# Half-row matmul pieces, a split cell and a new written order in a row-LSTM kernel

## The chip, the cores and the metric

The kernel runs on one core of one Trainium2 chip. The metric is the device time of one execution in microseconds (us), as the median of several executions. The engines are called as the profile calls them: PE (TensorE matmul) with PEld (its weight loads), DVE (VectorE), ACT (ScalarE), POOL (GpSimd) and SP (SyncE, which issues the DMAs).

## The reference

The input x has 8 images of 96 channels, 128 rows and 128 columns, in fp32. It is group-normalised (32 groups), a masked 1x3 convolution turns each row into 4x96 gate inputs, and an LSTM runs down the 128 rows. Its state h is convolved along the row with a full 3-tap kernel. The output is x plus h.

```
its = conv(gn(x), W_is * mask) + b_is            # 1x3, causal mask
def step((h, c), row):
    gates = conv1d(h, W_ss) + b_ss + row         # 3 taps, 96 -> 384
    f, i, o = sigmoid(three of the four parts);  g = tanh(the fourth)
    c = f * c + i * g
    h = o * tanh(c)
out = x + h of all rows
```

Row r cannot begin its convolution of h before row r-1 has ended its output product.

## The kernel before

**Half steps.** The 8 images are two halves of 4 (s = 0 and 1). One row of one half is a half step, numbered n = 2*row + s, so there are 256. Half step n needs h of half step n-2. The two halves alternate, so that the pointwise work of half step n-1 can lie beside the matmuls of half step n.

**Products.** A half step has three PSUM banks, A, B and C (128 output channels each, 512 fp32 columns: even columns in the lower 256, odd ones in the upper 256). The 3-tap convolution is written as four products per bank on sums and differences of neighbouring columns: "1" takes `vs` (even plus odd), "2" takes `vf` (odd minus even), "0" and "3" take `vd` (two shifted differences). They contract over all 128 rows (96 channels of h and 32 of x). The remaining 64 channels of x come in as three "own" products per bank, P, Q and E, which contract over 64 rows: their operand `xs` and weights lie twice in SBUF, in rows 0-63 and in rows 64-127, and `own` picks one of the two copies by bank and half. All are made by `mm` (line 393), 256 columns each; each product is recorded as two weight loads and two matmuls[...].

**Pointwise work.** `copy` (cp) takes product 1 out with the bias; `even` (lo) and `odd` (hi) combine it with product 2 within the bank, on DVE; products 0, E and 3 are added to that by PE. Then `tanh` (ta) and `sigmoid` (si) run on ACT for each bank; `forget` (fg, f*c), `gated` (gt, i*g), `cell` (ce, the sum) on DVE, `cell_tanh` (th) on ACT, `output` (ou, o*th into `hx`) on DVE. From `hx`, `difference` (F, line 503) and `total` (S, line 499) on DVE and `shifted` (D, line 507) on POOL make the operands `vf`, `vs` and `vd` of half step n+2. `residual` (re) on POOL adds h to x. POOL also normalises the next block's rows (`work`, called from `finish`), and `finish` issues the stores and loads of a block of four rows on SP's queue.

**What sets the order.** PE, ACT, DVE and POOL are under a manual schedule: each engine runs its instructions in the order in which the text `PERIOD` (line 586) names them, with `PRODUCTS` (line 590) in place of X for the own products. `do` (line 607) reads the text. A mark ' means half step n-1, + means n+1, * means n+2. So in one period the products of half step n are on PE while the cell of n-1 is on ACT and DVE, and ou', F', S' and D' come while PE does the own products. Semaphore waits between the engines are put in by the framework.[...]

**The tail.** The last half step (lines 837 to 847) already does `cell`, `cell_tanh` and `output` in two parts of two images each.

Of the kernel before, what the change touches and what calls it, by code (L numbers as in the profile page):

```python
# [8 lines left out]
AF = mybir.ActivationFunctionType  # L9
# [12 lines left out]
def kernel(  # L22
# [32 lines left out]
    nc = tc.nc  # L55
    B, C, H, W = x.shape
    P = 128
    NH = 2
    BH = B // NH
# [4 lines left out]
    C2 = 64  # L64
# [21 lines left out]
    wt = [tap[1], wm[:, 0, :], wm[:, 1, :], tap[2]]  # L86
    wo = [wx[:, 0, :], wx[:, 1, :], tap[3]]
# [73 lines left out]
    E = mybir.EngineType  # L161
# [5 lines left out]
    def bank(name):  # L167
        return ps_pool.tile([P, 512], F32, tag="ps", name=name)
# [57 lines left out]
    class Scale:  # L226


        def __init__(self, s, lo, hi, banks=None):
            n, self.name = hi - lo, f"{s}_{lo}"  # L230
            self.st, self.rstd, self.nmr = (
                st[s][:, lo:hi], rstd[s][:, :, lo:hi], nmr[s][:, :, lo:hi]
            )


            self.first, at = banks is None, 0 if banks is None else 3 * BH
            self.banks = banks or [bank(f"{name}{self.name}") for name in ("dm", "pv")]
            self.dm, self.pv = (
                own[:, at : at + i * n].rearrange("p (i b) -> p i b", i=i)
                for own, i in zip(self.banks, (3, 2))  # L240
            )
            self.pm = self.dm[:, 1:3, :]
            self.q, self.t, self.minus = (
                const.tile([P, *shape], F32, name=f"{name}{self.name}")
                for name, shape in (("q", [n]), ("t", [2, n]), ("minus", [2, n]))
            )
            for i in range(2):
                self.mm(self.pv[:, i, :], i, eps[:, 0:n], start=self.first and i == 0)

        def mm(self, o, i, rhs, start=False, stop=False):  # L250
            nc.tensor.matmul(o, gm[:, i, :], rhs, start=start, stop=stop, skip_group_check=True)
# [104 lines left out]
    last = NT * NH - 1  # L356
    order = {"A": 0, "B": 1, "C": 2}

    def gt(n, s, row, shape=(C, 2 * HB)):
        return g_pool.tile(list(shape), F32, tag=n, name=f"{n}_{s}_{row}")  # L360

    class HalfStep:


        def __init__(self, n):
            self.n, (self.row, self.s) = n, divmod(n, NH)
            self.ps, self.m1, self.moving, self.done, self.gates = {}, {}, {}, set(), None
            self.started, self.images = set(), {}
            self.hx = hx[self.s][self.row // R % 2][:, self.row % R]
            self.xs = xs[self.s][self.row // R % 2][:, self.row % R]  # L370
            self.c = cs[self.s].rearrange("p t b j -> p (t b j)")
# [14 lines left out]
        def mm(self, a, half, weights, rhs, rows=slice(0, P)):  # L386
            self.take_bank(a)
            new = a not in self.started
            self.started.add(a)

            lo, hi = self.images.get(a, (0, BH))
            cols = slice(lo * J, hi * J)
            nc.tensor.matmul(  # L393
                self.ps[a][:, bass.ts(half, HB)][:, cols],
                weights[rows, bass.ts(a, P)],
                rhs[rows, cols],
                start=new,
                stop=False,
                skip_group_check=True,
            )  # L400

        def own(self, a, i):

            low = a == order["A"] or (a == order["C"] and (self.s == 0 or (self.n, i) == (1, 2)))
            rhs = self.xs[:, i].rearrange("p b j -> p (b j)")
            self.mm(a, i % 2, wo[i], rhs, slice(0, C2) if low else slice(C2, P))

        def p_(self, a):
            self.own(a, 0)
# [5 lines left out]
        def t_(self, a):  # L415
            if 2 * self.row + self.s == last:
                self.mm(a, 0, wh, self.xs[:, 2].rearrange("p b j -> p (b j)"))
            else:
                self.own(a, 2)

        def m1_(self, a):
            self.mm(a, 0, wt[1], self.moving["vs"][:, 0])

        def m2_(self, a):
            self.mm(a, 1, wt[2], self.moving["vf"][:, 0])

        def m0_(self, a):
            self.mm(a, 0, wt[0], self.moving["vd"][:, 1])

        def m3_(self, a):  # L430
            self.mm(a, 1, wt[3], self.moving["vd"][:, 0])

        def copy(self, a):
            self.m1[a] = self.tile(f"m{a}", (P, HB))
            m1, column = self.ps[a][:, 0:HB], bias[:, a : a + 1]
            if a == order["A"] and self.n not in (0, 2):
                nc.vector.tensor_scalar(self.m1[a], m1, column, None, ALU.add)
            else:
                nc.scalar.activation(self.m1[a], m1, AF.Identity, bias=column)  # L439

        def even(self, a):
            nc.vector.tensor_add(self.ps[a][:, 0:HB], self.m1[a], self.ps[a][:, HB:])  # L442

        def odd(self, a):
            hi = self.ps[a][:, HB:]
            nc.vector.tensor_sub(hi, self.m1[a], hi)  # L446

        def tanh(self, a):
            nc.scalar.activation(self.g[a * 32 : (a + 1) * 32], self.ps[a][C:P], AF.Tanh)  # L449


        def sigmoid(self, a):
# [7 lines left out]
            if self.row > 0:  # L460
                nc.vector.tensor_mul(f, f, self.c)  # L461

        def gated(self):
            to = self.g if self.row > 0 else self.c
            nc.vector.tensor_mul(to, self.ps[1][0:C], self.g)


        def part(self, ap, lo, hi):
            return ap.rearrange("p (t b j) -> p t b j", t=2, b=BH)[:, :, lo:hi]
# [4 lines left out]
                nc.vector.tensor_add(c, f, g)  # L474

        def cell_tanh(self, lo=0, hi=BH):
            if lo == 0:
                self.th = self.tile("th")
            nc.scalar.activation(self.part(self.th, lo, hi), self.part(self.c, lo, hi), AF.Tanh)  # L479

# [60 lines left out]
    def shared(s, k, *images):  # L541
        return [(normalise_shared, nc.gpsimd, s, k, j, 0, R) for j in images]
# [12 lines left out]
    def work(n):  # L555
        if n < len(FIRST):
            return FIRST[n]
        row, s = divmod(n, NH)
        k, r = divmod(row, R)
        parts = []  # L560
        if r == R - 1 and k + 2 < NB:
            parts.append((own_image, s, k + 2, 0))
        elif r < R - 1 and k + 1 < NB:
            parts.append((own_image, s, k + 1, r + 1))
        if k + 1 < NB:
            parts += shared(s, k + 1, *SHARED[r])
        if r == R - 2 and k + 2 < NB:
            parts.append((load_rows, s, k + 2))
        return parts

    def finish(n):
        for part, *args in work(n):
            part(*args)
        row, s = divmod(n, NH)
        k, r = divmod(row, R)
        if r == R - 1:
            store(s, k, R - 1 if k + 1 == NB else 0, R)
            if k + 2 < NB:
                load(s, k + 2)
        elif r == R - 2 and k + 1 == NB:  # L580
            store(s, k, 0, R - 1)
# [2 lines left out]


    PERIOD = (
        "2A 1A siB' fg' 2B taB' cpA 1B loA 3C' cpB hiA 0C' loB 1C taC' hiB 2C siC' 0A gt'",
        "3A cpC ce' 0B loC th' hiC", "X", "ou' F' S' D' re'", "3B taA siA",
    )
    PRODUCTS = (  # L590
        "P+A P+B Q+A Q+B P+C P*A Q+C EA EB EC",
        "Q+A P+B P+C Q+B Q+C EB EA EC",
    )
    PARTS = {
        "P": "p_", "Q": "q_", "E": "t_", "1": "m1_", "2": "m2_", "0": "m0_", "3": "m3_",
        "cp": "copy", "lo": "even", "hi": "odd", "ta": "tanh", "si": "sigmoid",
# [7 lines left out]
            steps[n] = HalfStep(n)  # L604
        return steps[n]

    def do(n, names):

        for name in names.split():
            at = n  # L610
            for mark, offset in (("'", -1), ("+", 1), ("*", 2)):
                if mark in name:
                    at, name = n + offset, name.replace(mark, "")
            tile_ = name[-1] if name[-1] in order else ""
            part = name[: len(name) - len(tile_)]

            if part in ("S", "F", "D"):
                at += NH
            if not 0 <= at <= last:
                continue  # L620
            step = half_step(at)
            if name not in step.done:
                step.done.add(name)
                getattr(step, PARTS[part])(*([order[tile_]] if tile_ else []))

# [117 lines left out]
    n = m = 0  # L745
    for b in range(B):
# [7 lines left out]
        for k in range(QW // CH):  # L754
# [11 lines left out]
            if alone:  # L766
                i = list(shares).index(k)
# [12 lines left out]
    rows = ring[2][:, 0 : (R - 1) * BH * (W + 1)].rearrange("p (r q) -> p r q", q=W + 1)  # L780
# [12 lines left out]
    j = BH - 1  # L793
# [8 lines left out]
    step = half_step(1)  # L802
# [25 lines left out]
    finish(0)  # L828
    do(1, "gt th 0+A 3+A 0+B 3+B 0+C 3+C ou F S D re")
    finish(1)  # L830
    do(2, "taA siA P+C P*A Q+C")
    for n in range(3, last + 1):
        for names in PERIOD if n < last else PERIOD[:1]:
            do(n, PRODUCTS[n % 2] if names == "X" else names)
            if "re'" in names.split():
                finish(n - 1)
    do(last, "3A EA cpC ce' taA siA 0B 3B EB loC hiC th' siB taB fg ou' re'")
    finish(last - 1)
    do(last, "0C 3C EC taC siC gt")
    step, halves = half_step(last), [(0, BH // 2), (BH // 2, BH)]  # L840
    for at in halves:
        step.cell(*at)
# [60 lines left out]
```

## Time and profile before

| | before |
|---|---|
| median of 3 runs | 2062.54 us (2061.33 to 2066.29) |
| span of the profiled execution | 2059.9 us; its device time beside the span is not given, the runs lie 1.4 to 6.4 us above it |
| PE busy | 1961.9 us (95%), 10888 matmuls |
| DVE busy | 1675.9 us (81%) |
| ACT busy | 1363.7 us (66%) |
| POOL busy | 1449.6 us (70%) |
| granted TensorE clock | 0.997 |

Busy time is the time in which an engine had at least one instruction running. A timeline row gives the start, the time from the start of the first to the end of the last of the merged instructions, the engine, the line, what is written and read with its shape, and the number of instructions; in brackets stands how long the engine was idle before it and what ended that. For PE's matmuls the end is modelled, and successive matmuls overlap: what counts is the distance between their starts.

### The profile page before, as it was taken

The page shows a single profiled execution, that of the slowest core. Times are in us where ns is not written, and L with a number is a line of the kernel's source. Part 1 is how long each engine was busy: PE and PEld are TensorE (multiplying, and loading weights), DVE is VectorE, ACT ScalarE, POOL GpSimd, SP SyncE. Part 2 cuts the span into 40 slices and gives each one's busy share as a digit, 9 for nine tenths or more (in the row PEclk, how much of TensorE's full clock was granted, in tenths as well). Part 3 has the DMA queues.
Part 4 walks back from the last instruction along what each step waited for, and adds up shares of the span by engine and source line. Part 5 has one row for each costly group of instructions (what it writes and reads, how often), then busy time and mean ns, then how long its engine had stood idle before and what let it go on. Part 6 is the DMA issues. An engine that isn't in the chain of part 4 may idle for free.

```text
span 2059.9 us, 31445 instructions
## 1 busy us (share of the span) xinstructions
PE 1961.9 (95%) x10888; PEld 1597.5 (78%) x10888; DVE 1675.9 (81%) x3489; ACT 1363.7 (66%) x2403; POOL 1449.6 (70%) x1652
## 2 busy tenths in 40 slices
PE   0399999999999999999999999999999999999998
PEld 0278888888888888888888888888888888888886
DVE  5778888888888888888888888888888888888887
ACT  4776666666666666666666666666666666666666
POOL 3358777777777777777777777777777777777762
PEclk9999999999999999999999999999999999999999
DMA  9994333344433334443333443333444333344411
GB/s 381 424 309 109 91 84 89 97 113 113 107 74 85 88 99 113 113 103 75 86 88 101 113 113 100 73 90 87 104 113 113 99 74 87 88 106 113 113 31 32
DMA packets 103326, 236.26 MB, mean 115 GB/s; under 512 B 5953, under 2 KB 8897, under 8 KB 97281
## 3 DMA queue, kind: packets, MB, share of 16 engines
q1 hardware_dynamic: 103168, 234.25, 41.8%
q8 instruction: 88, 1.44, 0.3%
q14 instruction: 70, 0.57, 0.1%
HBM read 183.90 MB, written 50.33 MB: 114 GB/s over the span
## 4 chain that ended last, share of the span: by engine, by line
PE 93%; DMA 3%; DVE 2%; ACT 1%; POOL 0%; issue 0%; SPq 0%; DVEq 0%; POOLq 0%
PE ps L393 93%; DMA xs<-in_x_dram 3%; DVE bst L771 1%; POOL xw L297 0%; POOL xs L315 0%; POOL xs L316 0%; ACT piece L295 0%; SPq L759 0%; ACT piece L216 0%; ACT xs L216 0%; ACT xs L217 0%; ACT piece L217 0%; ACT g L449 0%; DVE st L677 0%; ACT th L479 0%
## 5 line engine op out<-in xcount | busy, mean ns | idle before, releaser
L393 PE MATMUL ps<-vd,wl 128*128 128x256 f32 x3072 | 814.3, 388 | 0.1
L449 ACT ACTIVATE g<-ps 32x512 f32<-32x512 f32 x768 | 454.3, 592 | 450.5 <-PE ps L393 442.4
L393 PEld LDWEIGHTS ps<-vd,wl 128*128 128x128 f32 x3072 | 562.4, 190 | 151.3 <-issue 84.7
L507 POOL TENSOR_TENSOR vd<-hx 128x512 f32<-128x512 f32 x257 | 266.5, 1037 | 459.0 <-DVE vs L499 457.8
L393 PE MATMUL ps<-xs,wx 64*128 64x256 f32 x3080 | 459.9, 394 | 11.0 <-POOL xs L315 11.0
L393 PE MATMUL ps<-vs,wm 128*128 128x256 f32 x1540 | 460.6, 381 | 4.0 <-POOL vs L499 4.0
L393 PE MATMUL ps<-vf,wm 128*128 128x256 f32 x1540 | 460.4, 381 | 0.0
L456 ACT ACTIVATE ps<-ps 96x512 f32<-96x512 f32 x766 | 417.7, 572 | 16.1
L393 PEld LDWEIGHTS ps<-xs,wx 64*128 64x128 f32 x3080 | 323.9, 187 | 119.7 <-issue 83.9
L461 DVE TENSOR_TENSOR ps<-ps,c 96x512 f32<-96x512 f32 x254 | 176.6, 695 | 259.4 <-ACT ps L456 259.4
L446 DVE TENSOR_TENSOR ps<-m,ps 128x256 f32<-128x256 f32 x768 | 329.1, 429 | 27.3 <-PE ps L393 1.2
L525 POOL TENSOR_TENSOR x<-x,hx 96x512 f32<-96x512 f32 x255 | 330.5, 1296 | 5.7 <-DVE hx L486 5.7
L442 DVE TENSOR_TENSOR ps<-m,ps 128x256 f32<-128x256 f32 x768 | 324.8, 423 | 9.7 <-ACT m L439 0.9
L393 PEld LDWEIGHTS ps<-vs,wm 128*128 128x128 f32 x1540 | 293.6, 191 | 45.9 <-POOL vs L499 5.0
L393 PEld LDWEIGHTS ps<-vf,wm 128*128 128x128 f32 x1540 | 293.9, 191 | 41.1 <-POOL vf L503 0.5
L439 ACT ACTIVATE m<-ps,wl 128x256 f32<-128x256 f32 x514 | 243.9, 475 | 74.8 <-PE ps L393 61.5
L316 POOL TENSOR_TENSOR xs<-xw 128x512 f32<-128x512 f32 (+1 forms) x254 | 270.4, 1064 | 0.0
L393 PE MATMUL ps<-xs,wt 64*128 64x256 f32 x1530 | 264.6, 377 | 0.0
L479 ACT ACTIVATE th<-c 96x512 f32<-96x512 f32 (+1 forms) x257 | 161.4, 628 | 104.8 <-DVE c L474 103.8
L297 POOL TENSOR_SCALAR hx<-x,rstd,nmr 32x512 f32<-32x512 f32 (+1 forms) x252 | 204.7, 812 | 25.9
L297 POOL TENSOR_SCALAR xw<-xr,rstd,nmr 128x512 f32<-128x512 f32 x252 | 204.8, 813 | 8.1 <-DVE nmr L289 6.5
L393 PEld LDWEIGHTS ps<-xs,wt 64*128 64x128 f32 x1530 | 195.0, 187 | 18.1 <-issue 0.7
(91 smaller groups left out, 1295.2 us busy)
## 6 DMA issues: line engine op xcount, KB each, us to landing
xr<-in_x_dram SPq DMA_DIRECT2D x124, 512.0 KB, 6.7
x<-in_x_dram SPq DMA_DIRECT2D x63, 768.0 KB, 5.9
out_dram<-x SPq DMA_DIRECT2D x62, 768.0 KB, 4.9
xs<-in_x_dram SPq DMA_DIRECT2D x30, 1024.0 KB, 12.3
piece<-in_x_dram SPq DMA_DIRECT2D x16, 1024.0 KB, 12.3
x<-in_x_dram SPq DMA_DIRECT2D x62, 256.0 KB, 3.2
xs<-in_x_dram SPq DMA_DIRECT2D x4, 512.0 KB, 8.3
out_dram<-x SPq DMA_DIRECT2D x2, 576.0 KB, 3.8
```

The lines of the kernel that those rows point to most:

```text
L297: engine.tensor_scalar(dst, src, scale, shift, ALU.mult, ALU.add)
L316: nc.gpsimd.tensor_sub(differences, strided(xw[:, 0, :], 0, [(W + 1, n), (J, 2), (1, J)]), strided(xw[:, 0, :], J + 1, [(W + 1, n), (0, 2) ...
L393: nc.tensor.matmul(self.ps[a][:, bass.ts(half, HB)][:, cols], weights[rows, bass.ts(a, P)], rhs[rows, cols], start=new, stop=False, skip_g ...
L439: nc.scalar.activation(self.m1[a], m1, AF.Identity, bias=column)
L442: nc.vector.tensor_add(self.ps[a][:, 0:HB], self.m1[a], self.ps[a][:, HB:])
L446: nc.vector.tensor_sub(hi, self.m1[a], hi)
L449: nc.scalar.activation(self.g[a * 32 : (a + 1) * 32], self.ps[a][C:P], AF.Tanh)
L456: nc.scalar.activation(gate, gate, AF.Sigmoid)
L461: nc.vector.tensor_mul(f, f, self.c)
L479: nc.scalar.activation(self.part(self.th, lo, hi), self.part(self.c, lo, hi), AF.Tanh)
L507: diff = nc.gpsimd.tensor_sub(self.operand("vd", 2)[:, :, lo:hi], strided(h, 1, [(BH * JP - 1, 2), (JP, hi - lo), (1, J)]), strided(h, 0, ...
L525: (nc.gpsimd if 2 * row + s < last else nc.vector).tensor_add(xo, xo, self.h)
```

## The change

All products of h become two pieces of 64 rows each, one in rows 0-63 and one in rows 64-127, so that one half step has 24 such pieces and 9 own products, 33 in all. A small class `Lanes` gives each piece a row half in turn: an own product takes whichever half has had fewer, the second piece of a product takes the other half than the first. Before a piece that goes into a bank whose last piece was on the other row half, `lanes.wait` puts a no-operation on PE that waits for that last piece's end, unless a later piece has been waited for already.

The gate product, the cell, its tanh, the output and the tanh of bank C are made in two parts of two images ("b" is images 2 and 3, "a" is 0 and 1). The copy of bank A moves from DVE to ACT. `re` is named one period later (re''), and `work` of half step n-1 (W) no longer comes after the residual but by itself. D is named at the start of the next period (D''), S and F at the end of the period, after the output. `PRODUCTS` is gone; there is one text for all periods. The last half step's E remains a full 128-row product, as do its products 0 and 3 where neither piece has been made.

```diff
+    class Lanes:
+        ROWS = (slice(0, C2), slice(C2, P))
...
+        def take(self, first=None):
+            if first is not None:
+                self.last = 1 - self.ROWS.index(first)
+            elif self.taken[0] != self.taken[1]:
+                self.last = int(self.taken[1] < self.taken[0])
+            else:
+                self.last = 1 - self.last
+            self.taken[self.last] += 1
+            return self.ROWS[self.last]
...
+        def wait(self, number):
+
+            if number > self.waited:
+                tc.add_manual_dep(
+                    nc.tensor.nop().ins,
+                    self.made[number].ins.name,
...
+                self.waited = number
...
             cols = slice(lo * J, hi * J)
-            nc.tensor.matmul(
+            before = self.writer.get(a)
+            if before is not None and before[0] != rows and whole not in (before[0], rows):
+                lanes.wait(before[1])
+            made = nc.tensor.matmul(
...
+            self.writer[a] = rows, lanes.issued(made)
...
+        def piece(self, kind, a):
+
+            if kind in OWN:
+                i, rows = OWN[kind], lanes.take()
+                self.mm(a, i % 2, wo[i], self.xs[:, i].rearrange("p b j -> p (b j)"), rows)
+                return True
+            first = self.halves.pop((kind, a), None)
+            rows = lanes.take(first)
+            half, i, (name, part) = H_PRODUCTS[kind]
+            self.mm(a, half, wt[i], self.moving[name][:, part], rows)
+            if first is None:
+                self.halves[kind, a] = rows
+            return first is not None
...
-            if a == order["A"] and self.n not in (0, 2):
+            if a == order["A"] and self.n in (1, last):
                 nc.vector.tensor_scalar(self.m1[a], m1, column, None, ALU.add)
...
         def even(self, a):
+            self.writer.pop(a, None)
             nc.vector.tensor_add(self.ps[a][:, 0:HB], self.m1[a], self.ps[a][:, HB:])
...
-        def tanh(self, a):
-            nc.scalar.activation(self.g[a * 32 : (a + 1) * 32], self.ps[a][C:P], AF.Tanh)
+        def tanh(self, a, lo=0, hi=BH):
+            g, ps = self.g[a * 32 : (a + 1) * 32], self.ps[a][C:P]
+            nc.scalar.activation(self.part(g, lo, hi), self.part(ps, lo, hi), AF.Tanh)
...
-        def gated(self):
+        def gated(self, lo=0, hi=BH):
             to = self.g if self.row > 0 else self.c
-            nc.vector.tensor_mul(to, self.ps[1][0:C], self.g)
+            to, i, g = (self.part(ap, lo, hi) for ap in (to, self.ps[1][0:C], self.g))
+            nc.vector.tensor_mul(to, i, g)
...
     PERIOD = (
-        "2A 1A siB' fg' 2B taB' cpA 1B loA 3C' cpB hiA 0C' loB 1C taC' hiB 2C siC' 0A gt'",
-        "3A cpC ce' 0B loC th' hiC", "X", "ou' F' S' D' re'", "3B taA siA",
+        "2A hiC' siA' D'' 1B 1A taA' 2B fg' 3C' 1A 0C' re'' taB' 2A 2B EC' 1B cpA 0C' 2C W loA cpB "
+        "3C' 1C siB' loB PB+ QA+ hiA taCb' 2C hiB taCa' 0A gtb' 1C siC' gta' EA 0B ceb' cpC 3A PA+ "
+        "cea' thb' PC+ 3B loC tha' QC+ oub' EB oua' QB+ 3A F' 3B 0A S' 0B"
     )
-    PRODUCTS = (
-        "P+A P+B Q+A Q+B P+C P*A Q+C EA EB EC",
-        "Q+A P+B P+C Q+B Q+C EB EA EC",
-    )
+    IMAGES = {"a": (0, BH // 2), "b": (BH // 2, BH)}
+    SPLIT = ("taC", "gt", "ce", "th", "ou")
...
-    do(2, "taA siA P+C P*A Q+C")
-    for n in range(3, last + 1):
-        for names in PERIOD if n < last else PERIOD[:1]:
-            do(n, PRODUCTS[n % 2] if names == "X" else names)
-            if "re'" in names.split():
-                finish(n - 1)
-    do(last, "3A EA cpC ce' taA siA 0B 3B EB loC hiC th' siB taB fg ou' re'")
-    finish(last - 1)
-    do(last, "0C 3C EC taC siC gt")
+    for n in range(2, last + 1):
+        do(n, PERIOD, by_lanes=True)
+    do(last, "cpA cpB cpC loA hiA loB hiB loC hiC 0A 3A EA 3B 0B EB", by_lanes=True)
+    do(last, "taA siA 0C 3C EC siB taB fg taC siC gt oua' oub' re'", by_lanes=True)
```

## The prediction, made before the result was known

> **What bounds the kernel now.** I read the page's busy shares and chain first, then the waits, then one period of PE, ACT and DVE in the timeline.
>
> ```profile
> PE 1961.9 (95%) x10888; PEld 1597.5 (78%) x10888; DVE 1675.9 (81%) x3489; ACT 1363.7 (66%) x2403; POOL 1449.6 (70%) x1652
> ...
> PE 93%; DMA 3%; DVE 2%; ACT 1%; POOL 0%; issue 0%; SPq 0%; DVEq 0%; POOLq 0%
> ```
>
> PE is the chain for 93% of the span. A period has 42 recorded matmuls (21 products of two). The S of 1005.82 us and the last one at 2043.68 are 138 half steps apart: 7.52 us per half step. Where does it go?
>
> ```profile
> PEld ps L393 <- issue: 169.3, 511, 0.3
> ```
>
> This row of the waits (total, times, longest) says that the weight loads stood still some 0.33 us, 511 times, for nothing that the profile shows: twice per half step. The timeline of one period shows where:
>
> ```profile
> 1002.60 1.46 PE L393 MATMUL ps<-vd,wl 128*128 128x256 f32 x6
> ...
> 1003.98 1.17 PEld L393 LDWEIGHTS ps<-xs,wx 64*128 64x128 f32 x12 [0.33 <-issue]
> 1003.99 1.57 PE L393 MATMUL ps<-xs,wx 64*128 64x256 f32 x12
> ...
> 1006.34 0.30 PEld L393 LDWEIGHTS ps<-vd,wl 128*128 128x128 f32 x2 [0.33 <-issue]
> 1006.34 0.70 PE L393 MATMUL ps<-vd,wl 128*128 128x256 f32 x2
> 1006.88 0.59 PE L393 MATMUL ps<-vf,wm 128*128 128x256 f32 x2
> ```
>
> Six full-row matmuls take 1.46 us: starts are 0.216 apart (5 x 0.216 + 0.38). Twelve half-row ones take 1.57, as six steps of two: the row halves run side by side. At each change of height a start comes 0.31 after the last instead of 0.22 (the last full-row one starts at 1003.68, then 1003.99), and the first matmul holds 0.10 to 0.11 more (0.70 against 0.59 for two). A change costs 0.197. Check: 24 full-row matmuls x 0.216 = 5.18, nine own products x 2 / 2 x 0.2157 = 1.94, two changes 0.39: **7.51 us**, against 7.52. PE never waits for data; the cell is hidden.
>
> **What the Trainium skill says.** "TensorEngine Tiling (Array Packing)", Key Properties: changing the tiling mode drains TensorE, and tiles run independently. The trace agrees, with 0.197 and the pairs above. "PSUM — Partial Sum Buffer", on bank collisions: two TensorE writes from different row tiles into one bank raise an error, hence the no-operations; no run here shows one, since before each bank's own products keep to one half. "VectorE: DVE Perf Modes", Two Vector instructions with no wait between them: a next instruction that isn't held starts before the one in front is finished. The trace agrees:
>
> ```profile
> 1001.51 0.43 DVE L446 TENSOR_TENSOR ps<-m,ps 128x256 f32<-128x256 f32 x1
> 1001.85 0.42 DVE L442 TENSOR_TENSOR ps<-m,ps 128x256 f32<-128x256 f32 x1
> ...
> 1004.76 0.68 DVE L486 TENSOR_TENSOR hx<-ps,th 96x512 f32<-96x512 f32 x1
> 1005.47 0.43 DVE L503 TENSOR_TENSOR vf<-hx 128x256 f32<-128x256 f32 x1
> 1005.82 0.42 DVE L499 TENSOR_TENSOR vs<-hx 128x256 f32<-128x256 f32 x1
> ```
>
> Independent 256-column operations start 0.34 apart although each lasts 0.43; F, which reads the output, starts 0.03 after its end.
>
> **Part 1, matmuls.** 33 pieces x 2 matmuls / 2 halves x 0.2157 = **7.11 us** per half step, with no change of height: 0.39 below now, 100 us over 254 periods. That is the most there is to gain. I worked the turns of `take` through PERIOD: they alternate strictly, and there are seven no-operation waits per period, four on the piece three back, one five back, two seven back. Their price is in no row. A piece's second matmul starts 0.22 after its first and is seen by ACT 0.44 later (E of bank A at 1005.60, tanh at 1006.04); with 0.05 to a weight load and 0.10 to its stream, a piece starts 0.81 after the piece waited for. Three back is 0.43 or 0.86, or 0.65 where the halves are skewed. I take nothing for the even-distance ones, and count the others where they fall. Bounds: zero, and 0.1 per period on the path.
>
> **Part 2, the cell.** Now the loop that had slack must be measured, because F', S' stand at the end of the text and 2A, 1B of the next period at its head: the 2.4 us of own products that covered F and S are gone. F releases 2A; PE's order puts 2A, 1A, 3C', 0C', 2B and the second 1B on the same row half; that releases cpB, then loB, and behind it DVE has hiA hiB gtb' gta' ceb' cea' loC oub' oua' F', which releases the next 2A. This is one loop per period:
>
> - F's end to the weight load 0.05 (the S ending at 137.30 releases a load at 137.35), to the stream 0.10.
> - Five pieces ahead of the second 1B on its half: 5 x 0.431 = 2.16. Its second matmul 0.22, to ACT 0.44.
> - cpB on ACT 0.475 (the row of line 439), to DVE 0.03.
> - loB to oub': eight starts x 0.34 = 2.72. ACT's parts fit: taCb' ends 0.8 after cpB, gtb' needs it 1.0 after; tha and thb take 0.42 each behind ceb and cea.
> - oub' to oua': 0.53. The tail of this kernel has this very pair:
>
> ```profile
> 2053.91 0.75 DVE L474 TENSOR_TENSOR c<-ps,g 96x256 f32<-96x256 f32 x2
> 2054.82 0.95 DVE L486 TENSOR_TENSOR hx<-ps,th 96x256 f32<-96x256 f32 x2 [0.15 <-ACT th L479]
> ```
>
>   Two cell halves of 0.42 take 0.75: 0.33 apart. Two output halves of 0.42 take 0.95: 0.53 apart. The second tanh was done at 2055.12, yet the second output starts at 2055.34, after the first one's end (2055.24). The second waits for the first; I take it that their interleaved rows in `hx` count as overlapping.
> - oua' to F' 0.45, F' 0.43.
>
> Sum: 0.15 + 2.16 + 0.66 + 0.475 + 0.03 + 2.72 + 0.53 + 0.88 = **7.61 us**. This is over 7.11, so PE will wait in front of 2A, and over 7.52. A second place agrees: 0A waits for hiA (0.43 + 0.34 after loB's start) and so begins about 0.4 later than PE could; the 15 pieces after it still end before the next F. Before, the same loop came to some 6.7, because full-row 2A, 1A, 2B, 1B need 1.73 with nothing in between; it was hidden.
>
> **The other edits.** The copy of A on ACT takes 0.48 from DVE and adds 0.475 to ACT; the halves add 0.07 to 0.15 per pair to DVE and ACT. Per period DVE comes to about 6 of 7.61 and ACT to 5.5: neither is full, but DVE's last 4 us are all on the loop. POOL keeps its 5.7 us (D 1.04, re 1.30, normalising 3.3); D'' now starts right at S' and ends 3 us before 0A wants it; re'' and W behind it cost nothing while POOL's idle 1.9 us stand, and if that cover went D would be late and 0A with it. W waits for EC', the last reader of the operands that it overwrites, at about 2.5 us of the period. On SP's queue the store follows re'', one period later, and the loads follow the store: 4.9 to land it and 3.2 for the next rows, some 8 us, against 10 until POOL reads them; two us of cover, once in eight half steps. PC+ waits for gta' about 0.1. Start and tail: I take zero, within 5 us.
>
> **Sum.** 7.61 - 7.52 = 0.09 on 253 periods: +22 us. On the profiled execution 2059.9 becomes 2082; the median of the runs is 2.6 above that span, so **2085 us**.
>
> **Rivals.**
> 1. *The output halves aren't tied.* Then oua' follows at 0.34, the loop is 7.42 and the time 2062.5 - 25 = 2037. For it: cell and tanh halves are not tied. Against: the tail row. Place: oub' to oua'; price 0.19; it decides the sign, as the loop need only lose 0.09.
> 2. *The loop isn't closed as I think* (the halves run ahead of each other, or a wait I counted isn't there), and PE's 7.11 plus small stalls of 0.15 sets the end: 7.26, 1997. For it: the order spaces the pieces of a bank. Against: each link is a data dependence or one engine's order.
> 3. *The waits are dear.* 1A, 2B and EC', all ahead of the second 1B, carry no-operations; 0.035 or more each on its half gives 7.72: 2113.
> 4. *The change does nothing for PE*: 64-row pieces don't pair or still drain. The row of twelve speaks against it; I give it 0.02 within rival 3's side.
> 5. *Errors cancel*, within 0.3%: 7.50 to 7.55.
>
> **Chances.** Forecast 2070 to 2106: 0.50; rival 1: 0.13; rival 2: 0.16; rivals 3 and 4: 0.11; rival 5: 0.10. About 0.3% (6 us) is what a measurement can tell from no change. Faster 0.29, same 0.10, slower 0.61. The range reaches down to rival 1 with 5 us for start and tail, 2030, and up to the dear waits, 2112; left out are rival 2 and the worst of 3 and 4. The likeliest case's own range is 2070 to 2106.
>
> **What would show it.** Right: no 0.33 us "issue" rows in PEld; instead once per period PE waits for DVE's F or S, and again for hiA; pairs of half-row matmuls 0.216 apart; DVE back to back from loB to S; L486 pairs of 0.95; S 7.6 us apart. Wrong: S under 7.5 apart, output pairs of 0.75, or PE without idle time. The prediction is wrong if the loop has a link less.

## The result and the profile after

| | before | after |
|---|---|---|
| median of 5 runs each | 2062.02 us (2061.28 to 2066.29) | 2070.66 us (2069.58 to 2070.98) |
| span of the profiled execution | 2059.9 us | 2069.1 us |

The change makes the kernel slower by a little: the medians differ by 8.6 us, and the ratio is 1.0039 with a 95% interval of 1.0026 to 1.0051. The forecast was 2085 us: the side is right, the size is not.

The busy shares and the chain of the changed kernel:

```profile
PE 1968.3 (95%) x16936; PEld 1855.3 (90%) x16936; DVE 1549.1 (75%) x3996; ACT 1494.3 (72%) x3161; POOL 1448.2 (70%) x1652
...
PE 93%; DMA 4%; ACT 2%; DVE 1%; issue 0%; SPq 0%; POOL 0%; DVEq 0%; POOLq 0%
```

They read as before: PE busy for 95%, PE the chain for 93%. But they no longer mean that PE is the bound. Two row halves now run side by side, independently, as the Trainium skill ("TensorEngine Tiling (Array Packing)", Key Properties) says of tiles; the trace agrees, the halves' starts lie 0.04 us apart ahead of 2A's wait and 0.10 to 0.12 after it. PE counts as busy while either of them streams. The steady part, from 700 to 1900 us, has these waits (total, times, longest):

```profile
ACT ps L525 <- PE ps L440: 219.6, 159, 1.4
...
PEld ps L440 <- issue: 22.9, 119, 0.2
```

The "issue" rows of 0.33 us, twice per half step, are gone with the changes of height. No row says that PE waits for DVE. What bounds it is seen in one period of the timeline, of DVE, ACT and PEld in turn:

```profile
1000.48 0.96 DVE L510 TENSOR_TENSOR ps<-m,ps 128x256 f32<-128x256 f32 x2 [0.82 <-ACT m L506]
1001.35 0.75 DVE L514 TENSOR_TENSOR ps<-m,ps 128x256 f32<-128x256 f32 x2
1002.01 0.74 DVE L535 TENSOR_TENSOR g<-ps,g 96x256 f32<-96x256 f32 x2
1002.67 0.74 DVE L544 TENSOR_TENSOR c<-ps,g 96x256 f32<-96x256 f32 x2
1003.34 0.41 DVE L510 TENSOR_TENSOR ps<-m,ps 128x256 f32<-128x256 f32 x1
1003.66 0.94 DVE L556 TENSOR_TENSOR hx<-ps,th 96x256 f32<-96x256 f32 x2
1004.63 0.43 DVE L573 TENSOR_TENSOR vf<-hx 128x256 f32<-128x256 f32 x1
...
1007.98 0.96 DVE L510 TENSOR_TENSOR ps<-m,ps 128x256 f32<-128x256 f32 x2 [0.81 <-ACT m L506]
```

```profile
1007.48 1.00 ACT L506 ACTIVATE m<-ps,wl 128x256 f32<-128x256 f32 x2 [0.42 <-PE ps L440]
```

```profile
1001.88 0.18 PEld L440 LDWEIGHTS ps<-vd,wl 64*128 64x128 f32 x1 [0.19 <-issue]
...
1005.11 0.29 PEld L440 LDWEIGHTS ps<-vf,wm 64*128 64x128 f32 x2
```

This is the predicted loop. F (L573) ends at 1005.06; 0.05 later the load of 2A begins, and only then its half of the rows has work again. The other half is still busy with product 3, so that no idle time is written down. Five pieces later the copy of B ends on ACT, loB (the second of the two L510) begins 0.03 behind it, and DVE runs without a gap from loB to F. The row at 1001.88 is 0A behind hiA; PEld's 0.19 of idle time there is called "issue", though it waits for DVE: in each of the 160 half steps from 700 to 1900 us the load starts 0.12 after an end of L514. The output pair is 0.94 long, the cell pair 0.74. All this was in the forecast. The period wasn't: S starts lie 7.50 us apart in six of eight half steps and 7.57 in two, against the forecast 7.61. The mean is 7.522, and before it was 7.520.

So the steady part gained and lost nothing. The 9.2 us of span lie at the ends, by the starts of S (numbered from 1 in order of time; numbers 3 and 4 are the two parts of one S, and from number 5 on there is one per half step):

| stretch | before | after | difference |
|---|---|---|---|
| to S number 4 (no edit is in force yet) | 137.07 | 138.36 | +1.3 |
| S 4 to 10 | 49.18 | 53.31 | +4.1 |
| S 10 to 16 | 45.05 | 45.82 | +0.8 |
| S 16 to 257 | 1812.38 | 1812.83 | +0.5 |
| S 257 to the end | 16.22 | 18.80 | +2.6 |

The first line isn't the change's: over all kernels of this study S 4 starts between 136.5 and 140.0, with the same code up to there (139.96 for the kernel before with one more operation from half step 4 on). S 4 to 5 takes 12.8 in both. In the six half steps after S 5 the kernel before needs 6.6 to 8.1 us each. PE bounds it there too, and some products were made ahead: between S 5 and 6 it has some 20 whole matmuls and 16 of own products to do, against 24 and 18 in the steady part. The changed kernel needs 7.5 to 8.8: never less than its loop, and in four of the six more. The trace shows two extra causes. From 150 to 192 us the weight loads wait three times for PE's own earlier pieces, 1.3 us in all. Only the no-operations make PE wait for itself:

```profile
PEld ps L440 <- PE ps L440: 1.3, 3, 0.5
```

The other is in DVE's and POOL's rows:

```profile
158.40 1.13 DVE L573 TENSOR_TENSOR vf<-hx 128x256 f32<-128x256 f32 x1
```

```profile
158.18 1.06 POOL L316 TENSOR_TENSOR xs<-xw 128x512 f32<-128x512 f32 x1
```

F takes 1.13 us in place of 0.43. It ends at 159.53, 0.29 after the POOL instruction that was running when it began. The same happens to the F at 198.91 (1.15 us), so that by the 0.7 that each F is longer some 1.4 us of the 4.9 lie here (an estimate). The second order below shows the cause.

### The profile page after: what moved, and what is told of

It reads as the page before. It is cut to its first block, busy times and chain, and to the rows that moved or that the text cites. A ratio compares the mean times of both kernels' runs of the same rounds, so it can differ in the third digit from the quotient of the medians.

```text
span 2069.1 us, 45097 instructions
## 1 busy us (share of the span) xinstructions
PE 1968.3 (95%) x16936; PEld 1855.3 (90%) x16936; DVE 1549.1 (75%) x3996; ACT 1494.3 (72%) x3161; POOL 1448.2 (70%) x1652
## 4 chain that ended last, share of the span: by engine, by line
PE 93%; DMA 4%; ACT 2%; DVE 1%; issue 0%; SPq 0%; POOL 0%; DVEq 0%; POOLq 0%
PE ps L440 92%; DMA piece<-in_x_dram 3%; DMA xs<-in_x_dram 1%; ACT piece L216 1%; PE ps L174 0%; ACT piece L217 0%; DVE bst L861 0%; ACT hx L295 0%; ACT piece L295 0%; DVE hx L556 0%; ACT xs L216 0%; ACT xs L217 0%; SPq L849 0%; DVE ps L514 0%; PE pv L251 0%
## 5 line engine op out<-in xcount | busy, mean ns | idle before, releaser
L440 PE MATMUL ps<-vd,wl 64*128 64x256 f32 (+1 forms) x6096 | 1391.2, 380 | 0.5 <-DVE ps L514 0.3
L440 PEld LDWEIGHTS ps<-vd,wl 64*128 64x128 f32 (+1 forms) x6096 | 1029.1, 186 | 64.3 <-issue 38.1
L440 PE MATMUL ps<-vs,wm 64*128 64x256 f32 (+1 forms) x3052 | 827.2, 392 | 4.4 <-POOL vs L569 4.4
L440 PE MATMUL ps<-vf,wm 64*128 64x256 f32 (+1 forms) x3052 | 806.7, 385 | 0.3 <-DVE vf L573 0.3
L440 PE MATMUL ps<-xs,wx 64*128 64x256 f32 x3080 | 650.0, 377 | 11.1 <-POOL xs L315 11.1
L440 PEld LDWEIGHTS ps<-xs,wx 64*128 64x128 f32 x3080 | 506.4, 188 | 14.2 <-POOL xs L315 11.6
L510 DVE TENSOR_TENSOR ps<-m,ps 128x256 f32<-128x256 f32 x768 | 325.4, 424 | 238.9 <-ACT m L506 213.8
L518 ACT ACTIVATE g<-ps 32x256 f32<-32x256 f32 (+1 forms) x1021 | 468.2, 481 | 26.9 <-PE ps L440 6.5
L440 PEld LDWEIGHTS ps<-vf,wm 64*128 64x128 f32 (+1 forms) x3052 | 475.3, 187 | 10.2 <-DVE vf L573 1.0
L440 PEld LDWEIGHTS ps<-vs,wm 64*128 64x128 f32 (+1 forms) x3052 | 440.6, 186 | 25.0 <-POOL vs L569 5.4
L440 PE MATMUL ps<-xs,wt 64*128 64x256 f32 x1530 | 456.2, 379 | 0.3 <-DVE ps L514 0.2
L514 DVE TENSOR_TENSOR ps<-m,ps 128x256 f32<-128x256 f32 x768 | 301.3, 423 | 1.3 <-PE ps L440 1.2
L556 DVE TENSOR_TENSOR hx<-ps,th 96x256 f32<-96x256 f32 (+1 forms) x510 | 212.2, 416 | 28.4 <-ACT th L549 1.5
```

Of the source, the lines that this page charges most:

```text
L440: made = nc.tensor.matmul(self.ps[a][:, bass.ts(half, HB)][:, cols], weights[rows, bass.ts(a, P)], rhs[rows, cols], start=new, stop=False, ...
L518: nc.scalar.activation(self.part(g, lo, hi), self.part(ps, lo, hi), AF.Tanh)
L556: nc.vector.tensor_mul(self.h[:, :, lo:hi], o, th)
```

## The experiments

The kernels ran in four groups, each group on one chip with runs of the kernel before beside it, whose medians were 2062.38, 2062.27, 2062.08 and 2062.08 us. The ratios are against these.

### Is the loop through F the bound? One more operation on it, in both kernels

```
         def difference(self, engine=nc.vector, lo=0, hi=BH):
             e, o = self.pair(lo, hi)
+            if self.n > 3 and engine is nc.vector:
+                engine.tensor_sub(self.operand("vs")[:, 0, lo:hi], o, e)
             self.last = engine.tensor_sub(self.operand("vf")[:, 0, lo:hi], o, e)
```

What it writes is overwritten by S. In the changed kernel:

> The changed kernel with one more 128x256 subtraction on DVE ahead of F in every half step from n = 4 on; it writes the tile that S then overwrites. Theory (the loop from F over 2A, 1B, cpB, loB and the gate work back to F sets the period): F comes 0.34 us later in each turn, the period goes from 7.50 to 7.84, 252 x 0.34 = 86 us more than the changed kernel, about 2156 us. Rival (PE sets the period by its own pace, 7.11 us of pieces and 0.39 of stalls at the waits between the row halves): the work hides, within 10 us of the changed kernel's 2071.

Measured: 2154.71 us, ratio to before 1.0447 (1.0431 to 1.0462). Predicted by the loop theory: 2156. The period is 7.837, 0.333 more, which is the distance of two starts on DVE:

```profile
1002.52 0.43 DVE L574 TENSOR_TENSOR vs<-hx 128x256 f32<-128x256 f32 x1
1002.86 0.42 DVE L575 TENSOR_TENSOR vf<-hx 128x256 f32<-128x256 f32 x1
```

Every nanosecond on this path is paid for. In the kernel before:

> The same extra subtraction in the kernel before. Theory: its loop has some 0.8 us of slack behind the own products on PE, so 0.34 us of DVE costs nothing: within 4 us of 2062. If the loop bound this kernel too, it would be 86 us more, 2148 us.

Measured: 2077.57 us, 1.0072 (1.0055 to 1.0089). It isn't the 2148 of a loop-bound kernel, but neither is it 2062. From 700 to 1900 us PE now has a wait that wasn't there:

```profile
PEld ps L393 <- issue: 104.8, 316, 0.3
PEld ps L393 <- DVE vf L505: 10.1, 20, 0.5
```

Twenty times in 159 half steps, one in eight, the load of 2 waits 0.5 us for F. That is 16 us over the whole span, the 15 measured. But it is not the 0.34 of the added operation that makes PE wait. In 118 half steps of this stretch the operation takes 0.43, and PE waits for F in none of them. In the other 40 it begins while POOL is normalising, takes 0.79 to 0.91 and ends 0.28 after POOL's instruction. All twenty waits are among these 40:

```profile
735.37 1.72 POOL L297 TENSOR_SCALAR hx<-x,rstd,nmr 32x512 f32<-32x512 f32 x2
736.46 0.91 DVE L504 TENSOR_TENSOR vs<-hx 128x256 f32<-128x256 f32 x1
737.76 0.30 PEld L393 LDWEIGHTS ps<-vf,wm 128*128 128x128 f32 x2 [0.55 <-DVE vf L505]
```

The section on the second order takes this up. The slack itself was smaller than the 0.8 that I gave it: in the kernel before, the load of 2A starts 0.35 to 0.42 after F's end in half of the half steps and 0.70 to 0.77 in the others, and 0.05 is the least that any run shows. So the slack is 0.30 to 0.37 or 0.65 to 0.72, and 0.34 more just fits.

### Cutting the loop

```
-            self.mm(a, half, wt[i], self.moving[name][:, part], rows)
+            rhs = wl[:, 0:HB] if kind in "12" and self.n > 3 else self.moving[name][:, part]
+            self.mm(a, half, wt[i], rhs, rows)
```

With a constant operand the recurrence through products 1 and 2 is left out.

> The changed kernel, but products 1 and 2 of the half steps from n = 4 on read a constant tile in place of vs and vf, so that PE waits for neither F nor S; this leaves out the recurrence through those two products, and the output is not the reference's. All instructions stay. Theory: the loop is cut, PE runs at 33 pieces x 0.2155 = 7.11 us plus stalls at 0A and PC+ of up to 0.15: 7.11 to 7.26 a half step, 60 to 100 us less than the changed kernel, 1970 to 2010 us. Rival (PE's own waits set 7.50): no change, 2065 to 2075 us.

Measured: 2033.23 us, 0.9856 (0.9842 to 0.9871). That is 37 us less than the changed kernel, so the recurrence through F and S does hold it, and the rival falls. But it is 23 us above my range. The period is 7.31 to 7.34 in half of the half steps and 7.37 on average, not 7.11 to 7.26. 0A's load still stands still for hiA in every half step, for 0.13 to 0.21:

```profile
1006.10 0.18 PEld L440 LDWEIGHTS ps<-vd,wl 64*128 64x128 f32 x1 [0.21 <-issue]
```

and D waits for PE's last reads of `vd` in 82 half steps of 163. So a second bound, only 0.15 shorter on average, lies behind the first. Which of these waits makes it, this run doesn't tell.

### The two ends

The end first. My reason for its 2.6 us was the height: the last half step's own products are whole there and stand between pieces. All of them as pieces:

```
-                at < last or part in ("P", "Q") or (part, order[tile_]) in step.halves
+                at <= last
...
-    do(last, "taA siA 0C 3C EC siB taB fg taC siC gt oua' oub' re'", by_lanes=True)
+    do(last, "taA siA 0C 3C EC 0C 3C siB taB fg taC siC gt oua' oub' re'", by_lanes=True)
```

> The changed kernel with one edit at its end: the last half step's own products of kinds 0, 1, 2, 3 and E are written as 64-row pieces too, where the changed kernel has them as whole products between pieces of the half step ahead of it. Theory (the end of the changed kernel costs 2.6 us more than that of the kernel before because TensorE changes its row height there again and again): 1 to 2.5 us less than the changed kernel, about 2068.8 us. Rival (the end is bound by the chain of VectorE and ScalarE, whatever the height): within 0.5 us of 2070.7 us. The steady part is untouched: 7.504 us in six of eight half steps.

Measured: 2071.84 us, 1.0045 (1.0032 to 1.0058); S 257 to the end is 18.6. No gain: the reason as I put it falls. The chain at the end shows what came in place of the changes of height:

```profile
2059.83 0.04 issue
2059.87 0.71 PE ps L440 x2
2060.58 0.04 issue
2060.63 0.71 PE ps L440 x2
```

These are the no-operation waits. Here pieces of one bank follow each other directly on alternating row halves, and each waits until the one before is done: 0.75 us per piece, where pieces that pair take 0.2157. So the waits that were free in the period are not free as such. The opposite edit has the last period's products whole, as far as they have not begun:

```
-                at < last or part in ("P", "Q") or (part, order[tile_]) in step.halves
+                at < (last if n < last else last - 1) or part in ("P", "Q") or (part, order[tile_]) in step.halves
```

> The changed kernel with the opposite edit of the tail: in the last period the products of the last two half steps that have not begun as pieces are whole, so that nearly all of TensorE's last work is whole products and few changes of height are left. Theory (at the end it is TensorE's mixture of heights and its pieces that wait for one another which cost the 2.6 us): 16 to 17.5 us from the last total to the end of the span against 18.8 in the changed kernel, 1.3 to 2.8 us less in all, about 2068.6 us. Rival (the end follows from the halves in two parts on VectorE): 18.5 us or more, within 0.5 us of 2070.7 us.

Measured: 2069.42 us, 1.0034 (1.0022 to 1.0047), and 16.52 us from S 257 to the end. The trace gives back 2.3 of the 2.6 us. The medians differ by 1.2, a little less than expected, which the intervals alone would not tell from nothing. By the trace it was PE's mixture of heights and waits at the end, not the split cell.

Then the start: half steps 3 to 9 in the order and whole products of the kernel before, whose PERIOD and PRODUCTS are kept for them (here FIRST_PERIODS and PRODUCTS).

```
-    for n in range(2, last + 1):
+    do(2, "taA siA P+C P*A Q+C")
+    for n in range(3, 10):
+        for names in FIRST_PERIODS:
+            do(n, PRODUCTS[n % 2] if names == "X" else names)
+            if "re'" in names.split():
+                finish(n - 1)
+    for n in range(10, last + 1):
         do(n, PERIOD, by_lanes=True)
```

> The changed kernel with its half steps 3 to 9 in the written order and the whole products of the kernel before, and the changed kernel's order and pieces from half step 10 on. Theory (5 of the 9 us are lost in the first half steps, where the kernel before has products made ahead and is not held by the loop): about 5 us less than the changed kernel, 2065.5 us, range 2063.5 to 2067.5. Rival (the loss is in the steady part, or the new order pays the same when it begins later): within 1.5 us of 2070.7 us.

Measured: 2071.09 us, 1.0044 (1.0032 to 1.0057). The time didn't move, and by my own expectation that speaks for the rival. The starts of S say otherwise: S 4 to 10 takes 49.52 us (before 49.18, after 53.31), so the old order does save 3.8 us there. But S 10 to 16 takes 49.83 against 45.82: the switch between the two orders costs the same 4.0 back, with half steps of 9.0, 9.3 and 8.3 us. About half of these 4.0 us are again operations of DVE that POOL held up: S takes 1.28 and 1.29 at 205.15 and 214.17, and the loads that need it wait 1.7 us, with 0.3 more for an F of 0.89. So the loss in the first half steps is shown in the trace; that it can be recovered in this kernel is not.

### What the pieces are for

The products of 128 rows whole, in the changed kernel's order:

```
-            if by_lanes and (part in OWN or part in H_PRODUCTS) and (
+            if by_lanes and part in OWN and (
```

> The changed kernel's written order and halves in parts, but its products of 128 rows are issued whole, at the place of their first piece; only the own products stay 64 rows high, in the places that the order gives them. It tells what the pieces are worth to this order. By the figures of the kernel before (0.216 per matmul, 0.197 per change of the row height): the own products stand in five groups between whole products, so ten changes of height, 1.97; 24 whole matmuls 5.18; nine own products of two matmuls each, in four pairs and one alone at best, about 2.2 to 2.6. Sum 9.4 to 9.8 per half step, that is 1.9 to 2.3 more than 7.52, and 2510 to 2620 us in all. Rival (the height change is hidden when the queue is full, or the chain of VectorE bounds this order too): below 2200 us.

Measured: 2620.77 us, 1.2708 (1.2685 to 1.2731), a period of 9.74 (expected 9.4 to 9.8). PE's rows:

```profile
1000.71 0.70 PE L440 MATMUL ps<-vd,wl 128*128 128x256 f32 x2
1001.34 0.70 PE L440 MATMUL ps<-xs,wt 64*128 64x256 f32 x2
```

Two matmuls and a change of height take 0.63 us from start to start: 2 x 0.216 + 0.197. The price that I read off the kernel before holds in another kernel. So the changed kernel's order, with own products anywhere between the others, can be afforded only with the pieces.

### Another order, to shorten the loop

If the written order sets the time, another order must move it. Here evenC lies between the two outputs, where it hides their tie, and evenA stands ahead of evenB:

```
-        "2A hiC' siA' D'' 1B 1A taA' 2B fg' 3C' 1A 0C' re'' taB' 2A 2B EC' 1B cpA 0C' 2C W loA cpB "
...
+        "siA' hiC' 2A 2B 1A siB' 1B 3C' D'' taA' 2A fg' 0C' 1A W' 2B EC' 1B taB' 3C' cpA QB+ "
+        "2C cpB re'' PB+ taCb' loA 1C QA+ loB gtb' siC' EA 2C hiB taCa' ceb' 0A gta' hiA thb' 1C 0B "
+        "PA+ EB cea' oub' 3A cpC 3B 0A PC+ 3B loC tha' oua' F' QC+ 3A 0C S' 0B"
```

(`W'` prepares the rows one number earlier, as this text begins at another place in the period; two lines of `do` are changed to read it.)

> The changed kernel with the same pieces and parts in another written order, whose loop is shorter by my sum: after the second piece of product 1 of tile B come copy B, even B, then gated b, odd B, cell b, gated a, odd A, cell a, output b, even C and output a, so that even C lies between the two outputs and hides their tie. Loop: 0.16 from the difference to TensorE, 2.16 for five pairs of pieces, 0.216 for the second matmul, 0.414 to ScalarE, 0.473 copy, 0.033, nine VectorE starts of 0.332 (2.99), 0.457 from the last output's start to the difference, 0.426 for it: 7.33, and 0.07 in two half steps of eight: 7.35 on average against 7.52. Theory (the loop through VectorE's order is what bounds the changed kernel): 0.17 x 237 = 40 us less than the changed kernel, about 2030 us, range 2022 to 2042. Rival (the pieces themselves, with their waits between row halves, hold TensorE at about 7.5 whatever the order): 2062 to 2080 us.

Measured: 2056.48 us, 0.9971 (0.9960 to 0.9981). It is 14 us faster than the changed kernel and faster than the one before, so the rival is wrong; but it has a third of the 40 us. The period is 7.45 in the undisturbed half steps, not 7.33. ACT's and PEld's rows say why:

```profile
1006.54 1.06 ACT L525 ACTIVATE ps<-ps 96x512 f32<-96x512 f32 x2 [1.31 <-PE ps L440]
1007.62 1.21 ACT L518 ACTIVATE g<-ps 32x512 f32<-32x512 f32 x2
1008.86 0.84 ACT L506 ACTIVATE m<-ps,wl 128x256 f32<-128x256 f32 x2
```

```profile
1004.50 0.51 PEld L440 LDWEIGHTS ps<-vd,wl 64*128 64x128 f32 x5 [0.25 <-DVE ps L514]
```

A loop that I had not counted has closed: 3A waits for hiA, sigmoid A for 3A, and then sigmoid A and B, tanh A and B, copy A and B stand back to back, 2.7 us from the first start to the last. Both tanh and the copy behind them start only after the end of the one in front (0.59, 0.62 and 0.62 from start to start), while two sigmoids are 0.49 and two copies 0.37 apart. Then loB, five starts on DVE to hiA, 3A and its followers on PE, and sigmoid A again: 2.69 + 0.50 + 1.76 + 0.47 + 2.04, which is the 7.45 but for rounding.

All three edits together (old start, this order from half step 10, pieces in the tail):

> The three edits together: the last half step's own products as pieces, half steps 3 to 9 in the order and whole products of the kernel before, and the other order from half step 10. Theory (start, loop and end are separate terms, which add): the other order's time less the gains of the two edits at the ends, about 2030 - 5 - 2 = 2023 us, range 2014 to 2036; the part of the start may be smaller, since the shorter loop holds the first half steps less. Rival (the terms are not separate): more than 4 us off the sum of the three measured gains.

Measured: 2054.10 us, 0.9960 (0.9946 to 0.9974), the lowest median here, but far from 2023, as the order alone had already fallen short. Alone the three gave -14.2, +0.4 and +1.2 us; the sum would be 2058.1. The 4.0 between are at the very edge of what the rival named. The traces explain a part: S 4 to 16 takes 94.9 here and 97.6 with the order alone, and the switch to this order costs nothing (S 10 to 16 takes 45.4). S 16 to 257 is 2.7 shorter too, where both kernels have the same text; why is not shown.

### A second order, and POOL's place in it

```
+        "2A W' 2B re'' hiC' 1A 1B siA' 3C' 1A 2A fg' 2B cpA loA 1B 0C' cpB loB 2C EC' 1C "
+        "3C' D'' PA+ taCa' hiA hiB PB+ 1C QA+ 2C taCb' EA 0B 0A EB 3A gta' gtb' 3B siC' cpC cea' "
+        "ceb' tha' QC+ 3A loC 0C 0A thb' 0B oua' oub' QB++ 3B taA F' taB siB PC+ S'"
...
+    do(2, "QB+", by_lanes=True)
```

> A second other order of the same pieces and parts. In the first one a new loop had closed: ScalarE did sigmoid A, sigmoid B, tanh A, tanh B and copy A one behind another, each tanh only after the end of the one ahead of it (0.59 to 0.62 from start to start against 0.37 to 0.49 for others), and sigmoid A waited for product 3 of A, which waits for odd A. Here tanh A and tanh B of a half step stand before the next difference, copy A and B stand far from them, and the first pieces of products 1 and 2 are placed so that four and a half, not five, piece times lie between the difference and the second piece of 1B. Theory: the loop is 7.505 - 0.108 - about 0.03 = 7.37 in six of eight half steps, 0.07 more in two: 0.133 x 237 = 32 us less than the changed kernel, about 2039 us, range 2030 to 2054 as another loop may close. Rival (about 7.45 is what these engines give together with any order): 2054 to 2062 us.

Measured: 2279.38 us, 1.1054 (1.1039 to 1.1069). A miss by 240 us. The same with a whole tail:

> The second other order with the last period's products whole as far as they have not begun as pieces. Theory (loop and end add): the second order's time less the gain of the whole tail, 1 to 3 us, about 2037 us. Rival (the end has its own limit that no order of TensorE moves): within 0.5 us of the second order alone.

Measured: 2279.87 us, 1.1055 (1.1040 to 1.1070); no gain in the median, though S 257 to the end is 17.7 in place of 18.8. What went wrong stands in two rows, one of DVE and one of POOL:

```profile
1008.77 1.52 DVE L569 TENSOR_TENSOR vs<-hx 128x256 f32<-128x256 f32 x1
```

```profile
1008.48 1.53 POOL L595 TENSOR_TENSOR x<-x,hx 96x512 f32<-96x512 f32 x1 [1.99 <-DVE hx L556]
```

S takes 1.52 in place of 0.42. The residual, which this text places ahead of D, starts on POOL when the outputs are there, and that is just ahead of S. S ends 0.28 after it. F, which begins just ahead of the residual, keeps its 0.43, and the residual takes 1.53 in place of 1.29. From 300 to 1900 us S began during the residual 143 times and took 1.52 each time. In the other 48 half steps it was F that began during it, and F took 1.54 to 1.55, S 0.41. The Trainium skill, "SBUF — State Buffer", section "Who interferes with whom", says that VectorE reads a second SBUF input through a port that it shares with GpSimd, and that whichever starts first keeps it for its whole instruction. The trace agrees: F and S read two SBUF operands, and wait for an instruction on POOL that began before them. The added operation of the kernel before, and the slow F and S of the first half steps above, fit the same account. The DVE operations with an operand in PSUM run beside POOL unhindered (0.41 to 0.43 in the changed kernel's rows above). To test it, the residual and the preparation go behind D again, with the whole tail as in the last run:

```
-        "2A W' 2B re'' hiC' 1A 1B siA' 3C' 1A 2A fg' 2B cpA loA 1B 0C' cpB loB 2C EC' 1C "
-        "3C' D'' PA+ taCa' hiA hiB PB+ 1C QA+ 2C taCb' EA 0B 0A EB 3A gta' gtb' 3B siC' cpC cea' "
+        "2A 2B hiC' 1A 1B siA' 3C' 1A 2A fg' 2B cpA loA 1B 0C' cpB loB 2C EC' 1C 3C' D'' "
+        "re'' W' PA+ taCa' hiA hiB PB+ 1C QA+ 2C taCb' EA 0B 0A EB 3A gta' gtb' 3B siC' cpC cea' "
```

> The second other order with the residual and the next rows' preparation written behind D again, as the changed kernel has them, and with the whole tail. In the second order the residual stood ahead of the total: it starts on GpSimd when the outputs are done, just as VectorE starts the difference and the total, and one of these two took 1.52 us there, against 0.42, in each half step. Theory (that overlap is the whole of the 240 us that the second order lost, and its loop is the 7.37 that it was made for): 7.33 to 7.38 in six of eight half steps, 0.07 more in two, and 1 us at the tail: about 2038 us, range 2030 to 2052. Rival (the second order's loop is itself longer, through ScalarE or TensorE, by more than GpSimd's share): above 2062 us.

Measured: 2055.75 us, 0.9969 (0.9957 to 0.9981), 224 us less than with the residual in front.

```profile
1007.52 0.43 DVE L573 TENSOR_TENSOR vf<-hx 128x256 f32<-128x256 f32 x1
1007.87 0.42 DVE L569 TENSOR_TENSOR vs<-hx 128x256 f32<-128x256 f32 x1
```

S is at 0.42 again. The order itself fell short of its 2038: three quarters of the half steps alternate between 7.34, as intended, and 7.59, and the mean is 7.47, as it was with the three edits together (7.47) and with the first other order (7.48). So the rival of the second order, that about 7.45 is what these engines give with any order, stays open. In the long half steps the load of 2A starts 0.21 after F's end instead of 0.05. A half step has 33 pieces, an odd number, so the row half that is ahead changes from one to the next; I take this to be the cause, but it was not tried.

## Why the prediction was right or wrong

- **What bounds the kernel now: right.** A change of height at 0.197 also fits the whole-row run. That the loop was hidden is right; that it came to some 6.7 is not. F's end has 0.3 to 0.7 us to spare, not 0.8, so the loop there comes to 6.8 to 7.2 (an estimate: 7.52 less the spare time).
- **Part 1, matmuls: right as a floor, not reached.** The changes of height are gone, pieces pair, and PE's 7.11 (33 x 0.2157 is rather 7.12) bounds no run of this study. The no-operation waits at zero: right for the steady part of this order, where five pieces take 2.158 with nothing between them and no row shows a wait of PE for itself. In the first half steps they cost 1.3 us, and where a bank's pieces follow each other a piece takes 0.75.
- **Part 2, the cell: the mechanism right, the terms too large.** The loop, its place, the tie of the outputs and 0A behind hiA are all in the trace, and one more operation cost what the loop said. The sum was 7.61 and measures 7.505:

| term | predicted | measured |
|---|---|---|
| F's end to PE's stream | 0.15 | 0.159 |
| five pieces | 2.16 | 2.158 |
| second matmul, to ACT | 0.66 | 0.630 |
| copy B, to DVE | 0.505 | 0.506 |
| eight DVE starts | 2.72 | 2.656 |
| output b to output a | 0.53 | 0.513 |
| to F, F | 0.88 | 0.883 |

  The **failed term** is the eight starts: I took 0.34 for each from pairs of 128 rows in the kernel before, and they are 0.332 on average here. With 0.03 at PE to ACT and 0.017 at the tie the loop is 0.1 shorter. That is 1.4% of it, and more than the whole forecast effect of 0.09: the sum was a difference of two nearly equal numbers.
- **A wait not counted:** in two half steps of eight F starts 0.07 later, as it also waits there for x that POOL has normalised. That brings the mean to 7.522.
- **The other edits at nothing: right** for residual and preparation behind D in the steady part. The second order shows what that place is worth: 224 us. But the reason that I gave, that D would be late, isn't what it showed: ahead of D the residual holds up S and F themselves. That POOL can hold up DVE stood in no term of the prediction.
- **"Start and tail: I take zero, within 5 us": wrong.** This is the second **failed term**. They come to some 7.5 us, outside what I allowed: 4.1 and 0.8 in the first half steps, 2.6 at the end. I had looked at the steady part alone.
- **The sum.** Predicted +22. The loop's error takes away 0.088 x 253 = 22, and start and end (with 1.3 of chance ahead of the edit) bring 9. (The 2.6 between span and median should have been 1.8, by which each run of the changed kernel lies above its own span.) The side came out right by the part that I had set to zero, which is luck. Of my rivals, "errors cancel" described the steady part, with 7.52.

## What to carry to other kernels

When a change moves the bound from an engine to a loop through several, add up the loop from start-to-start distances of the same instructions and give the sum an error: an estimate that is good to 1.5% cannot tell the sign of an effect of 1.2%. Then price the first and last periods separately, since products made ahead and the last step's order can be worth more than what the steady part gains. Write GpSimd's instructions where no VectorE operation with two SBUF operands on the loop can begin during them. And read a busy share of TensorE with two row halves with care: it stays at 95% while one half waits in every period.

## What was not expected of the hardware

- A VectorE addition or subtraction with two SBUF operands that begins during a long GpSimd instruction ends 0.28 us after it: 1.52, 1.13 and 0.91 us for an operation of 0.42.
- On ScalarE some instructions start only after the end of the one in front, and it isn't the function that decides. In the changed kernel the two tanh of bank C, which read the same rows and write the same rows, are 0.65 long together and 0.285 apart; those of A and B, which write to different rows, are 1.21 long and 0.615 apart. A copy behind a sigmoid waits for its end too (0.60 apart, at 1002.16 and 1002.76), though two copies (0.37) and two sigmoids (0.49) overlap. The trace shows no wait for the copy. A change of the first row, against the last instruction that read or wrote the same memory, would fit all of these, but no run changed the rows alone, so the cause stays open.

```profile
1001.48 0.65 ACT L518 ACTIVATE g<-ps 32x256 f32<-32x256 f32 x2
1002.16 0.57 ACT L525 ACTIVATE ps<-ps 96x512 f32<-96x512 f32 x1
1002.76 0.47 ACT L506 ACTIVATE m<-ps,wl 128x256 f32<-128x256 f32 x1
...
1005.85 1.21 ACT L518 ACTIVATE g<-ps 32x512 f32<-32x512 f32 x2
```

- Consecutive pieces of one bank on different row halves, each with its no-operation, take 0.75 us each.
